# Residual of the output added in PSUM and copied out by ScalarE, TensorE conv in one band of three, first LN1 in large buffers

## The chip, the cores and the metric

The kernel runs on one core of a Trainium2 chip, in one launch. The metric is the device time in microseconds. The core has five engines that each run their own instructions in order: TensorE (PE; its weight loads are listed as PEld), VectorE (DVE), ScalarE (ACT), GpSimd (POOL) and SyncE (SP). Sixteen DMA engines carry all transfers, whichever engine issues them. SBUF is the large on-chip memory; PSUM holds the results of TensorE in banks of 512 float32 per partition.

## The reference

The input x has 16 images of 128 channels and 96 x 96 pixels, all in float32. One transformer block is computed, and the LN weights are ones and the biases zeros in the inputs given.

```python
xn1 = _layernorm(x_hwc, ln1_w, ln1_b)                  # over the 128 channels of each pixel
q, k, v = (xn1 @ w.T for w in (wq, wk, wv))            # 8 heads of 16 channels
q, k = _l2norm(q), _l2norm(k)                          # over the 9216 pixels
attn = softmax(einsum('bhcn,bhdn->bhcd', q, k) * 16 ** -0.5)
x = x + (attn @ v) @ wp.T                              # channel attention: 16 x 16 per head
xn2 = _layernorm(x_hwc, ln2_w, ln2_b)
h1 = einsum('bchw,oc->bohw', xn2, w_in)                # 1x1 conv, 128 -> 512 channels
h2 = conv3x3_depthwise(h1, w_dw)                       # each of the 512 channels by itself
x = x + einsum('bchw,oc->bohw', gelu(h2), w_out)       # 1x1 conv, 512 -> 128
```

## The kernel before

Channels lie on the 128 partitions, pixels along the free dimension. An image is cut into 8 bands of 12 rows (1152 pixels); a band has 3 units of 4 rows (384 pixels). The kernel works through 128 bands (16 images of 8), and g counts them.

First norm and attention. A band of x is loaded (`load`, L540, issued by SP). Four tiles of 128 pixels (a quad) are transposed on TensorE (`forth`, L602), VectorE takes the statistics (L609), POOL makes variance and power (L616, L620), ScalarE scales the tiles (L647) into a buffer zT. For the first image VectorE scales two of the four (L634). There are three zT buffers, each for one quad. From zT TensorE sums the Gram matrix of the image (`gram`, L661) and transposes the tiles back to channels (`back`, L692), which ScalarE places (`place`, L698). The attention of an image (L756 to L852) is a chain of small steps on the Gram matrix that ends in one 128 x 128 matrix. `mix` (L560) multiplies it with the normed image; the residual x is added by VectorE for the first bands (L566), else by ScalarE's copy-out (L569) and an accumulating DMA of x from memory (`add_x`, L572, issued by POOL). A second norm of the same kind gives the input of the FFN.

FFN. The 512 hidden channels are four chunks of 128. A chunk in the usual way is a job (`conv_job`): `hidden` (L877) makes 14 rows of the hidden layer by matmuls of 480 or 384 columns, ScalarE copies them out of PSUM (`kept`, L882), and the nine taps of the depthwise conv are shared. VectorE does most taps, one instruction each over 1152 pixels (`tap`, L895). Two or three taps are done as products on ScalarE (`product`, L890) that accumulating DMAs add up, first onto each other and then onto VectorE's sum (`add_products`, L899, issued by POOL); chunk 1 has three such taps, the others two. ScalarE applies the gelu (L903). In some bands chunk 3 goes another way (`by_matmuls`): TensorE does the whole conv as nine matmuls per unit with weights that hold hidden layer and tap together (L945), and ScalarE applies the gelu out of PSUM (L951). `by_pe` picks these bands: of the first 120 every second one (`PE_OF = 2`), of the last eight the six in `PE_LAST`.

`ffn_out` ends a band: four matmuls per unit add the chunks up in PSUM (`product`, L968), VectorE adds x (`add`, L975), and SP stores the band (L979).

The order of the work. Each step is given to a planner (`Plan`) with its engine, an estimated duration, the tiles it reads and writes, and a place. The planner plays the engines through in time: a free engine takes the ready step with the lowest place. The place is the number of the job in whose turn the step lies, plus a constant for its kind from the table `AT`, so a very negative constant means "as soon as it is ready" and a large one "when nothing else is". The order found is written out and each engine keeps to it. `T_ADD` and `T_MOVE` are the planner's costs of an accumulating and a plain transfer. Buffers: four PSUM banks `h` shared by hidden rows, mix, conv and output, five product buffers `pr`, ten `h3` (the sum of taps of one chunk of a band), six x bands of the second phase.

```python
PE_OF = 2
PR_BUFS, H3_BUFS, ZT_BUFS = 5, 10, 3          # from a longer line
T_ADD, T_MOVE = 3100, 1800
k = NG - 1 - g
return k in PE_LAST if k < NB else k % PE_OF in PE_BANDS
```

Of the kernel before, what the change touches and what calls it, by code (L numbers as in the profile page):

```python
# [18 lines left out]
BR = 12  # L19
PE_CHUNK = 3  # L20
PE_BANDS = (0,)
PE_OF = 2
PE_LAST = (0, 1, 2, 4, 5, 7)
TINY = 1e-20
UNIT_MIN = 1e-18
# [3 lines left out]
QT, QB = 4, 1  # L29
# [1 line left out]
X1_BUFS, XB_BUFS, PR_BUFS, H3_BUFS, ZT_BUFS = 2, 6, 5, 10, 3  # L31
IN_TURN = ("tr", "h3", "pr", "xb", "x1")
AT = dict(
    weights=86, zeros=34, load_a=-17.95, forth_a=-1.35, stats_a=-23.85, variance_a=50.15, power_a=-16.45,
    scaled_a=6.1, gram=-31.8, back_a=-145.85, place_a=68, attention=-19.55, mix=-17.6, residual=60.15,
    mixed=-98.2, add_x=-22.85, forth_b=-2, stats_b=-5.55, variance_b=52.05, power_b=-11, shift_b=-76.95,
    scaled_b=98.5, back_b=-23.15, place_b=20.55, halo=21.65, hidden=1.35, kept=-79.55, products=8.4,
    add_last=-64.4, tap=0.1, add_first=-14.5, gelu=-63.5, conv=1.15, conv_gelu=-1.85, out=4.9, add=-43.45,
    store=47.1,
)  # L40
STEP = dict(scaled=0.3, hidden=0.1, products=0.5, tap=0.166, conv=1.6, conv_tap=0.03, out=0.8, out_part=0.05)
SLACK = 300
NORM1_END = 6.0
EARLY = 5
WAIT = dict(POOL=350, SP=1300, ACT=1300)
T_WEIGHTS = 20000
T_VARIANCE = 420
T_POWER = 1000
T_ADD, T_MOVE = 3100, 1800


class Plan:
# [154 lines left out]
def tile_restormer_block(  # L207
# [136 lines left out]
    )  # L344
    op = plan.op

    def at(kind, place):
        return place + AT[kind]

    def bank(key, n=4 * P):  # L350

# [7 lines left out]
    def t_mm(n):  # L359
        return 2 * max(110, 0.84 * n)  # L360
# [10 lines left out]
    def pe(ns, p, f, r, w):  # L371
        op("PE", ns, p, f, r, w, ns + 200 + SLACK, ns)

    def dve(ns, p, f, r, w, two=False):
        op("DVE", ns, p, f, r, w, ns + 120 + SLACK, ns + 120, two=two)
# [29 lines left out]
    def weights(p):  # L405
# [14 lines left out]
            nc.scalar.dma_start(out=v["win"], in_=w_in.rearrange("(n p) c kh kw -> p n (c kh kw)", p=P))  # L420
            nc.scalar.dma_start(out=v["wout"], in_=w_out.rearrange("c j kh kw -> c (j kh kw)"))

        def transposed(parts, kept, gives):

            key = ("weights", next(names))
            h = ("h", key)
            d = {}

            def forth():
                d["pt"] = bank(key)  # L430
                for k, part in enumerate(parts()):
                    nc.tensor.transpose(d["pt"][:, k * P : (k + 1) * P], part, ident)

            pe(440, at("weights", p), forth, mine, [h])
            dve(700, at("weights", p), lambda: kept(d["pt"]), [h], [("w", g) for g in gives] + mine[1:])

        def keep_qkp(pt):
            nc.vector.tensor_copy(v["wqkT"], pt[:, : 2 * P])
# [53 lines left out]
        def unit_parts():  # L492
            for n in range(NCH):
                nc.vector.tensor_scalar(v["wt"][:, n, :], v["win"][:, n, :], unit[:, n : n + 1], None, ALU.mult)

        op("ACT", 400, at("load_a", p), loads, [], mine, T_WEIGHTS, dma=2 * T_MOVE)
        dve(1400, at("weights", p), units, [], [("w", "in")])
        dve(400, at("weights", p), shifts, [], [("w", "in"), ("w", "conv"), ("w", "shift")])
        transposed(
            lambda: [v["wqk"][:, :P], v["wqk"][:, P:], v["wp"], wv_sb], keep_qkp, ["qk"]  # L500
        )
        pe(440, at("weights", p), biases, [("w", "qk"), mine[1]], [("h", ("weights", "biases"))])
        dve(400, at("weights", p), lambda: nc.vector.tensor_copy(cqk, v["pc"]), [("h", ("weights", "biases"))], [("w", "qk")])
        pc = ("h", ("weights", "centred"))
        pe(1000, at("weights", p), centred, [("w", "qk"), mine[1]], [pc])
        dve(800, at("weights", p), keep_centred, [pc], [("w", "qk")])
        dve(700, at("weights", p), unit_parts, [mine[0], ("w", "in")], [mine[1]])
        transposed(
            lambda: [v["wt"][:, n, :] for n in range(NCH)],
            lambda pt: nc.vector.tensor_scalar(winT.rearrange("p n c -> p (n c)"), pt, w2, None, ALU.mult), ["in"],  # L510
        )
        transposed(
            lambda: [v["wout"][:, n * P : (n + 1) * P] for n in range(NCH)],
            lambda pt: nc.vector.tensor_copy(woutT.rearrange("p n c -> p (n c)"), pt), ["out"],
        )
        for t0 in (0, 4, 8):
            ts = range(t0, min(t0 + 4, 9))
            dve(170 * len(ts), at("weights", p), lambda ts=ts: comp_parts(ts), [mine[0]], [mine[1]])
            transposed(
                lambda ts=ts: [v["wt"][:, t % 4, :] for t in ts],  # L520
                lambda pt, ts=ts: nc.vector.tensor_scalar(
                    comp[:, ts[0] : ts[-1] + 1, :].rearrange("p t c -> p (t c)"), pt[:, : len(ts) * P],
                    w2, None, ALU.mult,
                ), ["conv"],
            )
# [18 lines left out]
    def norm(i, second, place_of):  # L544
# [8 lines left out]
        def x2(s, u):  # L553
            d = {}
            b = u // UPB
            loaded = x_key(i, b, False) == "xb"

            def mix():
                pm = d["pm"] = bank((name, u), UT)
                nc.tensor.matmul(rows(pm), lhsT=mats[i][0], rhs=interior(i, u), start=True, stop=True)  # L560
                if (i, b) not in xbs:
                    xbs[i, b] = xpool.tile([P, BR * W], F32, tag="x", name=f"x2_{i}_{b}")

            def residual():
                xt = x_unit(xbs, i, u)
                nc.vector.scalar_tensor_tensor(xt, d["pm"], mats[i][1], xt, ALU.add, ALU.add)  # L566

            def mixed():
                nc.scalar.activation(x_unit(xbs, i, u), d["pm"], AF.Identity, bias=mats[i][1])  # L569

            def add_x():
                nc.gpsimd.dma_start(out=xbs[i, b], in_=x_band(i, b), accum_op=ALU.add)  # L572

            pm = ("h", (name, u))
            ins = [z_unit(i, u), ("m", i)]
            if loaded:
                pe(t_mm(UT), at("mix", s), mix, [*ins, xtok(u)], [pm])
                dve(t_dve(UT), at("residual", s), residual, [pm], [xtok(u)])
                return
            pe(t_mm(UT), at("mix", s), mix, ins, [pm, xtok(u)])  # L580
            act(t_act(UT, 1) - 43, at("mixed", s), mixed, [pm], [xtok(u)])
            if u % UPB == UPB - 1:
                xb = [xtok(b * UPB + k) for k in range(UPB)]
                add(at("add_x", s), add_x, [], xb)

        def pixels(s, m):

# [2 lines left out]
            early = i == 0 and (not second or m < EARLY)  # L590
            key_ = "h" if early else "tr"
            by_dve = QT // 2 if early else 0

            def forth(q):
                if early:
# [28 lines left out]
                nc.vector.scalar_tensor_tensor(nb, d["mv"][:, :, 1], -1.0, d["rstd"], ALU.mult, ALU.mult)  # L624

            def zT(q):
                zTs[q] = zT_bufs[plan.slot["zT", (name, q)]]
                return zTs[q]

            def also_scaled(q):  # L630
# [35 lines left out]
            trs, bt = [(key_, (name, q)) for q in qs], ("batch", (name, m))  # L666
            for q, tr in zip(qs, trs):
                units = {t // TPU: None for t in range(q * QT, (q + 1) * QT)}
                pe(110 * QT, at("forth" + ab, s), lambda q=q: forth(q), [xtok(u) for u in units], [tr])
            for j in range(QB * QT // 2):  # L670
                dve(341, at("stats" + ab, s), lambda j=j: stats(j), [trs[2 * j // QT]], [bt])
            op("POOL", T_VARIANCE, at("variance" + ab, s), variance, [], [bt], T_VARIANCE + 33 + SLACK)
            op("POOL", T_POWER, at("power" + ab, s), power, [], [bt], T_POWER + 33 + SLACK)
            if second:
                dve(80, at("shift" + ab, s), shift, [], [bt])
            for h, (q, tr) in enumerate(zip(qs, trs)):
                zt, sh = ("zT", (name, q)), s + STEP["scaled"] * h
                if by_dve:
                    dve(by_dve * 240, at("scaled" + ab, sh), lambda q=q: also_scaled(q), [tr, bt], [(*zt, 0)])
                act((QT - by_dve) * (343 if second else 250), at("scaled" + ab, sh), lambda q=q: scaled(q), [tr, bt], [(*zt, 1)])  # L680
                if not second:
                    pe(QT * 220, at("gram", sh), lambda q=q: gram(q), [(*zt, 0), (*zt, 1), ("w", "ones")], [("g", i)])

        def channels(s, u):

# [23 lines left out]

            pb = ("bk", (name, u))  # L710
            quads = {(u * TPU + j) // QT: None for j in range(TPU)}
            pe(110 * TPU, at("back" + ab, s), back, [("zT", (name, q), k) for q in quads for k in range(2)], [pb])
            act(t_act(UT, 1) - 43 if second else t_copy(UT), at("place" + ab, s), place, [pb, ("w", "shift")], [z_unit(i, u)])
            for k, r, row, of in copies:
                act(225, at("place" + ab, s), lambda k=k, r=r, row=row: place_row(k, r, row), [pb, ("w", "shift")], [("z", k, of)])


        for u in range(0, NU if not second else 0, UPB):
# [240 lines left out]
    def ffn_out(p, g, s):  # L959
        i, b = divmod(g, NB)  # L960
        d = {}
        po = ("h", ("out", g, s))
        order = sorted(range(NCH), key=lambda n: (n != PE_CHUNK, n))

        def product(k, n):
            if k == 0:
                d["po"] = bank(("out", g, s), UT)
            nc.tensor.matmul(  # L968
                rows(d["po"]), lhsT=woutT[:, n, :], rhs=h3s[g, n][:, s * UR : (s + 1) * UR, :],
                start=(k == 0), stop=(k == NCH - 1),  # L970
            )

        def add():
            xt = x_unit(xbs, i, s + b * UPB)
            nc.vector.tensor_add(xt, d["po"], xt)  # L975

# [4 lines left out]
        for k, n in enumerate(order):  # L981
            pk = p + STEP["out_part"] * k
            pe(t_mm(UT), at("out", pk), lambda k=k, n=n: product(k, n), [("h3", (g, n), s), ("w", "out")], [po])
        dve(t_dve(UT), at("add", p), add, [po], [("xb", (i, b), s)])
        if g == NG - 1:
            move(at("store", p), lambda: store(s, 1), [("xb", (i, b), s)], [], T_MOVE / UPB)
        elif s == UPB - 1:
            move(at("store", p), lambda: store(0, UPB), [("xb", (i, b), k) for k in range(UPB)], [], T_MOVE)

    def by_pe(g):  # L990
        k = NG - 1 - g
# [61 lines left out]
```

## Time and profile before

| what | value |
|---|---|
| time, median of 3 runs | 4176.35 us (4175.98 to 4178.71) |
| profiled execution | 4194.94 us, its span 4193.2 us |
| mean granted TensorE clock | 0.998 |
| PE, DVE, ACT, POOL busy | 99%, 97%, 88%, 62% of the span |
| moved by DMA | 827.63 MB, mean 197 GB/s |
| VectorE's additions of x (L975) | 384 of 558 ns |
| ScalarE's copies of hidden rows (L882, 384 columns) | 1118 of 508 ns |

The profile is one execution. Busy shares are averages over lead-in, steady work and tail. A row of the groups gives line, engine, operation, output and inputs, the count, then busy time and mean duration of one, then the idle time of the engine before them and what ended it. The duration of an instruction on TensorE, VectorE and ScalarE contains a part that the next instruction overlaps, so the pace of a run of equal instructions is read from their starts. A float32 matmul appears as two MATMUL rows. A share of the DMA queues is that of the time of all 16 engines.

### The profile page before, as it was taken

What the parts mean: (1) busy time and instruction counts of PE and PEld (TensorE: products, weight loads), DVE (VectorE), ACT (ScalarE), POOL (GpSimd) and SP (SyncE); (2) the same over time, 40 slices, a digit from 0 to 9 for tenths busy, and PEclk for the clock granted to TensorE, in tenths of its full rate; (3) what the DMA queues carried; (4) which work ended last, traced back from release to release, by engine and by line L of the source; (5) the groups of instructions that cost most, each with busy time, mean ns of one, the idle gap of its engine ahead of it and who ended that gap; (6) DMA issues with size and microseconds to landing.
All of it is one profiled execution on the core that took longest, in us unless ns stands there. A gap on an engine that the chain in (4) does not pass through costs nothing. (4 is left out here: it accounts for less than half of the span.)

```text
span 4193.2 us, 52283 instructions
## 1 busy us (share of the span) xinstructions
PE 4151.7 (99%) x17457; PEld 2684.0 (64%) x17457; DVE 4073.2 (97%) x4676; ACT 3682.0 (88%) x6970; POOL 2593.8 (62%) x2373
## 2 busy tenths in 40 slices
PE   8999999999999999999999999999999999999999
PEld 6666666666666666666666666666666666666565
DVE  6999999999999999999999999999999999999998
ACT  4988989899899888999988899898998989889885
POOL 3656666566675666657666566656656667565542
PEclk9999999999999999999999999999999999999999
DMA  2999999999999999999999999999999999999997
GB/s 78 192 191 201 208 198 208 189 213 201 206 207 204 206 196 204 203 202 207 198 206 198 197 206 198 206 201 201 208 197 212 195 207 202 191 205 199 196 197 160
DMA packets 203934, 827.63 MB, mean 197 GB/s; under 512 B 23568, under 2 KB 24976, under 8 KB 203664
## 3 DMA queue, kind: packets, MB, share of 16 engines
q0 software_dynamic: 164160, 672.47, 82.9%
q1 hardware_dynamic: 37152, 151.01, 9.8%
q8 instruction: 138, 2.26, 0.2%
q10 hardware_dynamic: 2352, 0.81, 0.1%
q14 instruction: 132, 1.08, 0.1%
HBM read 148.26 MB, written 75.50 MB: 53 GB/s over the span
## 5 line engine op out<-in xcount | busy, mean ns | idle before, releaser
L895 DVE SCALAR_TENSOR_TENSOR h<-h,ratio,h 128x1152 f32<-128x1152 f32 x2104 | 2933.0, 1415 | 5.0
L890 ACT ACTIVATE pr<-h,ratio 128x1152 f32<-128x1152 f32 x1018 | 1304.2, 1290 | 21.8 <-DMA pr<-pr 20.3
L945 PE MATMUL h<-xn,comp 128*128 128x384 f32 x3564 | 1277.4, 486 | 1.7 <-ACT h L951 0.9
L968 PE MATMUL h<-h,woutT 128*128 128x384 f32 x3072 | 1112.8, 487 | 1.8 <-ACT h L903 0.7
L877 PE MATMUL h<-xn,winT 128*128 128x384 f32 (+1 forms) x2676 | 1048.4, 500 | 2.1 <-DVE x L975 1.1
L945 PEld LDWEIGHTS h<-xn,comp 128*128 128x128 f32 x3564 | 647.3, 189 | 394.4 <-issue 10.4
L899 POOL DMA_DIRECT2D pr<-pr x573 | 545.7, 960 | 475.1 <-ACT pr L890 325.7
L968 PEld LDWEIGHTS h<-h,woutT 128*128 128x128 f32 x3072 | 560.7, 190 | 345.1 <-issue 7.5
L882 ACT COPY h<-h 128x384 f32<-128x384 f32 (+1 forms) x1338 | 658.1, 521 | 139.7 <-PE h L877 122.4
L877 PEld LDWEIGHTS h<-xn,winT 128*128 128x128 f32 x2676 | 479.5, 190 | 290.9 <-issue 49.7
L899 POOL DMA_DIRECT2D h<-pr x445 | 433.9, 977 | 356.7 <-DVE h L895 93.7
L895 DVE SCALAR_TENSOR_TENSOR h<-h,ratio 128x1152 f32<-128x1152 f32 x446 | 630.1, 1419 | 11.5 <-ACT h L882 7.8
L903 ACT ACTIVATE h<-h 128x1152 f32<-128x1152 f32 x448 | 533.7, 1192 | 51.9 <-DMA h<-pr 48.0
L616 POOL TENSOR_SCALAR ve_b<-st_b 128x4 f32<-128x4 f32 x288 | 364.3, 1265 | 310.8 <-DVE st_b L609 304.6
L620 POOL TENSOR_TENSOR rstd_b<-ve_b,mhalf 128x4 f32<-128x4 f32 x288 | 525.1, 1823 | 13.9
L620 POOL TENSOR_TENSOR rstd_a<-ve_a,mhalf 128x4 f32<-128x4 f32 x288 | 498.2, 1730 | 15.7 <-POOL ve_a L616 0.2
L616 POOL TENSOR_SCALAR ve_a<-st_a 128x4 f32<-128x4 f32 x288 | 323.9, 1125 | 292.2 <-DVE st_a L609 291.7
L651 ACT ACTIVATE zT<-pT_b,nb_b,rstd_b 128x128 f32<-128x128 f32 x1132 | 431.4, 483 | 45.7 <-DVE nb_b L624 45.4
L647 ACT ACTIVATE zT<-pT_a,rstd_a 128x128 f32<-128x128 f32 x1080 | 314.7, 398 | 39.3 <-POOL rstd_a L620 38.4
L661 PEld LDWEIGHTS g<-zT 128*128 128x128 f32 x2304 | 294.4, 192 | 50.0 <-ACT zT L647 7.9
L661 PE MATMUL g<-zT 128*128 128x129 f32 x2304 | 307.1, 276 | 3.3 <-ACT zT L647 3.3
L560 PE MATMUL h<-xn,mwT 128*128 128x384 f32 x768 | 283.5, 490 | 1.2 <-ACT x L569 0.8
(172 smaller groups left out, 3605.4 us busy)
## 6 DMA issues: line engine op xcount, KB each, us to landing
pr<-pr POOLq DMA_DIRECT2D x573, 576.0 KB, 6.9
h<-pr POOLq DMA_DIRECT2D x445, 576.0 KB, 7.4
x<-in_x_dram SPq DMA_DIRECT2D x128, 576.0 KB, 6.5
out_dram<-x SPq DMA_DIRECT2D x127, 576.0 KB, 5.6
x<-in_x_dram POOLq DMA_DIRECT2D x122, 576.0 KB, 7.7
out_dram<-x SPq DMA_DIRECT2D x3, 192.0 KB, 1.9
weights<-in_L_conv_w_in_dram ACTq DMA_DIRECT2D x1, 256.0 KB, 10.7
weights<-in_L_conv_w_out_dram ACTq DMA_DIRECT2D x1, 256.0 KB, 11.6
```

The source lines that it names most:

```text
L616: nc.gpsimd.tensor_scalar(ve, d["mv"][:, :, 2], 1.0 / C, EPS, ALU.mult, ALU.add)
L620: nc.gpsimd.tensor_tensor(rstd, d["ve"], mhalf, ALU.pow)
L651: nc.scalar.activation(zT(q)[:, k, :P], d["pT", q][:, k, :], AF.Identity, bias=d["nb"][:, t : t + 1], scale=d["rstd"][:, t : t + 1],)
L661: nc.tensor.matmul(grams[i][:, : P + 1], lhsT=zt[:, :P], rhs=zt, start=(q == 0 and k == 0), stop=(q == NU * TPU // QT - 1 and k == QT - 1),)
L877: nc.tensor.matmul(rows(ph), lhsT=winT[:, n, :], rhs=window(xn, r0 + r, e - r, 1), start=True, stop=True)
L882: nc.scalar.copy(window(h1_, r, e - r, 1), rows(d.pop(("ph", r))))
L890: nc.scalar.activation(to, shifted(t), AF.Copy, scale=ratio[:, n, t : t + 1])
L895: nc.vector.scalar_tensor_tensor(h3, shifted(t), ratio[:, n, t : t + 1], onto, ALU.mult, ALU.add)
L899: nc.gpsimd.dma_start(out=to, in_=d["pr", t], accum_op=ALU.add)
L903: nc.scalar.activation(h3, h3, AF.Gelu)
L945: nc.tensor.matmul(d["pc"], lhsT=comp[:, t, :], rhs=window(xn, r0 + dy, UR, dx), start=(t == 0), stop=(t == 8),)
L968: nc.tensor.matmul(rows(d["po"]), lhsT=woutT[:, n, :], rhs=h3s[g, n][:, s * UR : (s + 1) * UR, :], start=(k == 0), stop=(k == NCH - 1),)
```

## The change

1. The output's residual: for all bands but the last two, a fifth matmul adds x in PSUM, with the identity as weights, and ScalarE copies the sum out of PSUM over x. In the last two bands VectorE adds as before.
2. `PE_OF` goes from 2 to 3.
3. The first image's LN1: zT lies in the `h3` buffers (two quads in one) and not in the three zT buffers; POOL writes the column of ones in each.
4. The table of places is new: constants of their own for the first image (`_0`), for the load of the weights (`load_w`) and for the weights that the FFN needs (`late`). The planner's costs of transfers and of the weights' load are changed.

```diff
-PE_OF = 2
+PE_OF = 3
...
 AT = dict(
-    weights=86, zeros=34, load_a=-17.95, forth_a=-1.35, stats_a=-23.85, variance_a=50.15, power_a=-16.45,
...
-    add_last=-64.4, tap=0.1, add_first=-14.5, gelu=-63.5, conv=1.15, conv_gelu=-1.85, out=4.9, add=-43.45,
-    store=47.1,
+    load_w=-4.75, weights=-31.7, zeros=-128.5, load_a=-128.95, forth_a=-3.9, stats_a=-14.85, variance_a=359.5,
...
+    scaled_b=-72.8, back_b=-10.8, place_b=-110.1, res=-6.15,
+    evict_x=-72.85, halo=194.05, hidden=1.65, kept=27.1, products=9.4, add_last=-104.1, tap=7.9, add_first=7.45,
+    gelu=237.8, conv=0.8, conv_gelu=6.8, out=5.2, add=-34.55, store=254.3, mix_0=-15.9, residual_0=351.3,
...
-T_WEIGHTS = 20000
+T_WEIGHTS = 12000
...
-T_ADD, T_MOVE = 3100, 1800
+T_ADD, T_MOVE = 3060, 1640
...
             def zT(q):
-                zTs[q] = zT_bufs[plan.slot["zT", (name, q)]]
+                if q in zTs:
+                    return zTs[q]
+                if not apart:
+                    zTs[q] = zT_bufs[plan.slot["zT", (name, q)]]
+                    return zTs[q]
+                two = [k for k in (q - q % 2, q - q % 2 + 1)]
+                t = h3p.tile([P, BR * W], F32, tag="h3", name=f"zT_{two[0]}")
+                for k in two:
+                    zTs[k] = t[:, k % 2 * QT * (P + 1) : (k % 2 + 1) * QT * (P + 1)].rearrange("p (t c) -> p t c", c=P + 1)
+                    nc.gpsimd.memset(zTs[k][:, :, P:], 1.0)
                 return zTs[q]
...
+        by_pe_ = g < NG - 2
...
-                start=(k == 0), stop=(k == NCH - 1),
+                start=(k == 0), stop=(k == NCH - 1 and not by_pe_),
             )
 
-        def add():
+        def residual():
+            xt = x_unit(xbs, i, s + b * UPB)
+            nc.tensor.matmul(d["po"], lhsT=ident, rhs=xt, start=False, stop=True)
+
+        def evict_x():
+            nc.scalar.copy(x_unit(xbs, i, s + b * UPB), d["po"])
+
+        def add_here():
...
-        dve(t_dve(UT), at("add", p), add, [po], [("xb", (i, b), s)])
+        if by_pe_:
+            xt = ("xb", (i, b), s)
+            pe(t_mm(UT), at("res", p), residual, [xt], [po])
+            act(t_copy(UT), at("evict_x", p), evict_x, [po], [xt])
+        else:
+            dve(t_dve(UT), at("add", p), add_here, [po], [("xb", (i, b), s)])
```

## The prediction, made before the change was run

> **What bounds the kernel now.** I read the page's busy shares first. Three engines and the DMA are near full, so the shares alone decide nothing; I then cut the span into lead-in, middle and tail (columns: length, busy time of PE, PEld, DVE, ACT, POOL, granted clock, DMA share, GB/s).
>
> ```profile
> PE 4151.7 (99%) x17457; PEld 2684.0 (64%) x17457; DVE 4073.2 (97%) x4676; ACT 3682.0 (88%) x6970; POOL 2593.8 (62%) x2373
> ...
> q0 software_dynamic: 164160, 672.47, 82.9%
> q1 hardware_dynamic: 37152, 151.01, 9.8%
> ```
>
> ```profile
> 0.00:20.00 20.00, 8.88 (x46) 8.14 (x47) 7.72 (x32) 3.94 (x10) 6.45 (x24) 1.00 0.82 276
> 20.00:160.00 140.00, 129.16 (x710) 95.74 (x710) 113.18 (x222) 95.69 (x216) 70.48 (x107) 0.94 0.41 89
> 160.00:4150.00 3990.00, 3973.98 (x16582) 2557.20 (x16581) 3919.18 (x4394) 3566.14 (x6724) 2511.76 (x2237) 1.00 0.95 202
> ```
>
> In the middle TensorE idles 16 us of 3990, VectorE 71, ScalarE 424. TensorE sets the pace. Busy time of pipelined matmuls needs a check, so I read starts in the timeline of a middle stretch:
>
> ```profile
> 1004.22 2.42 PE L877 MATMUL h<-xn,winT 128*128 128x480 f32 x6
> 1006.48 2.10 PE L968 MATMUL h<-h,woutT 128*128 128x384 f32 x6
> 1008.41 1.45 PE L945 MATMUL h<-xn,comp 128*128 128x384 f32 x4
> 1009.70 0.49 PE L692 MATMUL pB_a<-ident,zT 128*128 128x128 f32 x3
> 1010.02 1.06 PE L661 MATMUL g<-zT 128*128 128x129 f32 x8
> ```
>
> Six 384-wide passes take 1008.41-1006.48 = 1.93 us, 0.322 each (the 486 ns of a row is latency). The first line holds the six passes of one 14-row band (four 480-wide, two 384-wide): 2.26 us. A 128-wide pass takes about 0.11. All passes: 9640 of 384 columns x 0.322 = 3104, 440 of 480 columns x 0.404 = 178, 6912 of 128 x 0.11 = 760, some 460 small ones of attention about 85: 4127 us, so the 4152 busy are truly filled.
>
> The Trainium skill (Perfetto Trace Analysis, Identifying the Most-Contended Engine) says that matmul busy time misjudges TensorE and that the share of weight loads should be used instead; that share is 64% here, and by it work taken off TensorE would be worth nothing (about 4170 us, the lead-in alone). The passes counted above say otherwise, and the measurement decides.
>
> **The change on TensorE.** Each matmul is two passes. Conv by TensorE falls from every second to every third of the first 120 bands: 60 to 40, 20 bands less (the last eight keep their six). Per band 9 taps x 3 units x 2 = 54 passes: -1080 x 0.322 = -348. Those bands' chunk 3 now needs its hidden rows: +20 x 2.26 = +45. The identity product: 126 bands x 3 units x 2 = 756 passes x 0.322 = +243. I take two passes, as the mix product L560 has (768 for 384 units), not one as the transposes have; one would make it 122 less. It waits for its x band, which the second norm has read long before. Sum **-60 us** on the path.
>
> **VectorE.** The addition L975 goes 378 times; next starts follow it by 0.46 us where I looked: -174. Twenty jobs of six taps come: a tap paces at (4.07-1.41)/2 = 1.33 us, +160. Sum -14: 3905 of the middle, nowhere the bound.
>
> ```profile
> 1008.56 4.07 DVE L895 SCALAR_TENSOR_TENSOR h<-h,ratio,h 128x1152 f32<-128x1152 f32 x3
> ```
>
> **ScalarE.** The copy-out is a form that the trace has (L698, 128x384 out of PSUM):
>
> ```profile
> L698 ACT COPY xn<-pB_a 128x384 f32<-128x384 f32 x384 | 194.7, 507 | 73.9 <-PE pB_a L692 72.9
> L890 ACT ACTIVATE pr<-h,ratio 128x1152 f32<-128x1152 f32 x1018 | 1304.2, 1290 | 21.8 <-DMA pr<-pr 20.3
> L951 ACT ACTIVATE h<-h 128x384 f32<-128x384 f32 x198 | 102.4, 517 | 44.2 <-PE h L945 43.8
> ```
>
> Back to back it paces at 0.37 us: 378 x 0.37 = 140 (192 by the row's mean). A moved band adds two products (1.15 each by starts), a gelu (1.07) and three evictions of hidden rows (1.24), and loses three conv gelus (0.39 each): 3.4 x 20 = 69. Sum +209: 3775 of the middle, 95%. Its 424 idle us are the cover. It frees every PSUM bank that TensorE fills in the FFN, and it runs in order: behind a late copy-out stand hidden-row evictions and products, and TensorE waits for banks. From below nothing (the copies fit the idle), from above half of the added 209 as TensorE waits; I take 5, since TensorE lost only 16 us in all with ScalarE at 89%.
>
> **DMA.** Each moved band adds two accumulating DMAs (products 1 and 2 of a two-tap job): 40. One costs 82.9% of 4193.2 / 1140 = 3.05 us of all 16 engines: **+122 us**. All queues hold 93.1% of the span, 3904 us; lead-in 16+57 and tail 23 taken off, the middle holds 3807, a share of 0.954. After: 3929. POOL issues them (some 0.97 us each, +39 on an engine at 62%); in POOL's queue the variance and power steps stand behind them, and the next norm waits for those.
>
> So in the middle TensorE needs 3974-60+16 = 3930 us if its idle stays, and DMA needs 3929 us if it never idles. The two meet. What DMA can hold is read from 50 us windows (three of eighty here, the same columns):
>
> ```profile
> 1260.00:1310.00 50.00, 50.00 (x192) 31.25 (x192) 49.36 (x61) 45.16 (x82) 24.66 (x25) 1.00 0.91 193
> 1310.00:1360.00 50.00, 50.00 (x198) 31.68 (x197) 49.60 (x55) 44.83 (x79) 28.99 (x27) 1.00 1.01 213
> 1360.00:1410.00 50.00, 50.00 (x216) 32.57 (x216) 49.06 (x54) 44.69 (x86) 34.75 (x30) 1.00 0.99 202
> ```
>
> Windows run from 0.85 to 1.02, and stretches at 1.00 go on without TensorE losing anything, so 0.95 is demand and not a ceiling. Middle by sustained share: 1.00 gives 3929 (-61), 0.9925 gives 3959 (-31), 0.985 gives 3989 (no gain), 0.975 gives 4030 (+40). I take 0.9925, halfway between full and break-even, because a fed queue shows 0.99 to 1.02, while five product buffers limit how much can be queued: median landing is already 6.9 to 7.4 us against 4.9 in the lead-in.
>
> [...]
>
> **Lead-in.** The first image's LN1 fills TensorE (19.60 of 20 us from 20 to 40: per quad 4 transposes, 8 Gram passes, 4 transposes back). Large buffers don't make passes cheaper; they let the 72 back-transposes (7.9 us) stand outside the chain to attention, whose serial steps at 51 to 66 us they can then fill. VectorE's first tap is at 97.3 us, the first accumulation at 102. Gain between 8 and -5 (ones columns written per buffer on POOL, and the weights hold two of ten buffers, so the last two quads wait for a release); I take -6 us. It is worth having for DMA too, which idles until then.
>
> **Other edits.** Every place in the order is changed, and the planner's transfer costs: 16 us of TensorE idle can be won, and nothing in the trace bounds the loss; nought is taken. Stores now wait for ScalarE, and x loads stand behind them on SP; that queue waits for buffers anyway, at no cost unless a copy-out is over a microsecond late.
>
> **Sum.** Profiled execution 4194.94 (span 4193.2 and 1.7 around it). Middle -31 (the 5 us of ScalarE waits lie inside DMA's limit), lead-in -6: 4158. The median is 0.9956 of the profiled time: 4176.35 - 37 x 0.996 = **4140 us**.
>
> **The rivals.**
> - TensorE alone sets the pace, DMA finds its room: middle 3930+5, lead-in -6: 4176 - 61 = 4115. For it: TensorE 99.6% full with VectorE at 98.2% beside it now. Against: DMA would be at 0.998.
> - DMA becomes the bound below 0.985, slower than before: its place is the chain of two or three dependent accumulations that each hold a product buffer; ScalarE's next product waits, and in order behind it everything that frees banks. At 0.975: 4176 + 40 - 6 = 4210. It decides from a sustained 0.985 downwards, 0.981 with the lead-in's gain. For it: gelu already waits 48.0 us for `h<-pr` and products 20.3 for `pr<-pr`. Against: these are small beside 3990.
> - ScalarE at 95% makes TensorE wait for banks by 55 us of the upper 105: the gain is gone, about 4170.
> - The reordering loses what the sums give; it has no row, and is in the range's upper end.
>
> **How the numbers follow.** Within 0.2% (8.4 us, about what this measurement can tell from none) is 4168 to 4184.7. Forecast (DMA and TensorE together, 0.987 to 0.997): 0.52, faster. TensorE alone: 0.18, faster. DMA below break-even: 0.20, of it 0.15 slower and 0.05 same. ScalarE or the order: 0.10, of it 0.02 faster, 0.05 same, 0.03 slower. Faster 0.72, same 0.10, slower 0.18. Low end: TensorE alone, with the 5 us of waits not lost and a lead-in of -11, 4176 - 71 = 4105. High end: a share of 0.978 (4017, +27), lead-in -3, 4200.
>
> **What would show it.** Right: 2484 conv passes, a new group of 756 identity passes, TensorE's total some 60 us lower, DMA share in the middle 0.98 or more, ScalarE about 95%, first tap some 6 us earlier. Wrong: a share that stays near 0.95 with TensorE idle after ScalarE (banks), gelu or products waiting hundreds of microseconds for DMA, an accumulation dearer than 3.05 us, or identity passes unlike 0.322 us.

## The result, and the profile after

The changed kernel takes 4220.39 us (4215.93 to 4222.51), the kernel before, run beside it, 4176.16 us (4175.24 to 4178.71). The ratio is 1.0103, 95% interval 1.0091 to 1.0115: slower by 44 us where 36 us faster was forecast, and above the high end of 4200.

The busy shares and DMA queues of the page after:

```profile
PE 4126.0 (98%) x17253; PEld 2645.1 (63%) x17253; DVE 4065.8 (96%) x4418; ACT 3871.2 (92%) x7408; POOL 2606.5 (62%) x2431
...
q0 software_dynamic: 169920, 696.07, 84.7%
q1 hardware_dynamic: 37152, 151.01, 10.0%
```

The pass count is the forecast one: 17457 - 1080 + 120 + 756 = 17253. VectorE has 258 instructions less but hardly less time. Now the same cuts as before (columns as there):

```profile
20.00:160.00 140.00, 130.88 (x759) 97.09 (x758) 117.81 (x225) 101.83 (x231) 72.65 (x110) 0.99 0.48 106
160.00:4150.00 3990.00, 3921.98 (x16256) 2502.38 (x16255) 3893.80 (x4125) 3733.74 (x7123) 2516.20 (x2267) 1.00 0.97 206
```

For comparison the kernel before must be taken from a second profiled execution. The first (4194.94 us) lies 18 us above the median of its runs; the second, of the run `before_again` below, has a span of 4174.8 us. The same stretch there:

```profile
160.00:4150.00 3990.00, 3981.77 (x16626) 2566.74 (x16625) 3930.24 (x4403) 3581.28 (x6734) 2482.49 (x2240) 1.00 0.96 202
```

TensorE was busy for all but 8 us of this middle; after, it idles 68 us, although ScalarE and DMA still show room (3734 of 3990, 0.97).

Busy time alone understates this, since after each interruption a matmul shows its whole 0.49 us, of which a run of them adds only 0.322 each. So I count TensorE's lost time: start of the last pass, minus start of the first, minus all passes at the prediction's paces (4127 us of work before, 4127 - 60 = 4067 after).

| kernel | TensorE work | first to last pass start | lost |
|---|---|---|---|
| before, first profile | 4127 | 5.6 to 4189.2 | 57 |
| before, second profile | 4127 | 5.4 to 4170.7 | 38 |
| after | 4067 | 5.6 to 4213.9 | 141 |

From the second profile of before to after, 60 us of work went and 103 us of lost time came: +43, the measured difference. What had to be found is where 103 us of waiting come from.

### The profile page after: what moved, and what is told of

It reads as the page before. It is cut to its first block, busy times and chain, and to the rows that moved or that the text cites. A ratio compares the mean times of both kernels' runs of the same rounds, so it can differ in the third digit from the quotient of the medians.

```text
span 4218.0 us, 52196 instructions
## 1 busy us (share of the span) xinstructions
PE 4126.0 (98%) x17253; PEld 2645.1 (63%) x17253; DVE 4065.8 (96%) x4418; ACT 3871.2 (92%) x7408; POOL 2606.5 (62%) x2431
## 3 DMA queue, kind: packets, MB, share of 16 engines
q0 software_dynamic: 169920, 696.07, 84.7%
## 4 chain that ended last, share of the span: by engine, by line
PE 54%; DVE 25%; ACT 12%; DMA 4%; POOL 3%; issue 2%; ACTq 0%; POOLq 0%; DVEq 0%
DVE h L917 22%; PE h L991 14%; PE h L967 12%; PE h L899 11%; ACT pr L912 4%; PE h L998 3%; PE g L677 3%; PE h L566 3%; DMA h<-pr 2%; ACT h L904 2%; PE pB_a L714 2%; PE pB_b L714 2%; PE pT_a L609 2%; PE pT_b L609 2%; ACT zT L667 2%
## 5 line engine op out<-in xcount | busy, mean ns | idle before, releaser
L917 DVE SCALAR_TENSOR_TENSOR h<-h,ratio,h 128x1152 f32<-128x1152 f32 x2204 | 3053.7, 1408 | 9.7
L912 ACT ACTIVATE pr<-h,ratio 128x1152 f32<-128x1152 f32 x1058 | 1391.7, 1320 | 40.9 <-DMA h<-pr 20.2
L967 PE MATMUL h<-xn,comp 128*128 128x384 f32 x2484 | 871.2, 486 | 2.5 <-ACT h L904 1.2
L991 PEld LDWEIGHTS h<-h,woutT 128*128 128x128 f32 x3072 | 561.1, 191 | 369.0 <-ACT h L904 23.1
L904 ACT COPY h<-h 128x384 f32<-128x384 f32 (+1 forms) x1398 | 700.7, 562 | 44.1 <-PE h L899 38.0
L921 POOL DMA_DIRECT2D h<-pr x465 | 473.5, 1025 | 274.7 <-DMA pr<-pr 61.5
L967 PEld LDWEIGHTS h<-xn,comp 128*128 128x128 f32 x2484 | 451.2, 189 | 281.5 <-issue 14.2
L925 ACT ACTIVATE h<-h 128x1152 f32<-128x1152 f32 x468 | 578.7, 1241 | 9.9 <-DMA h<-pr 8.0
L627 POOL TENSOR_TENSOR rstd_a<-ve_a,mhalf 128x4 f32<-128x4 f32 x288 | 538.1, 1869 | 13.8 <-POOL ve_a L623 0.2
L623 POOL TENSOR_SCALAR ve_b<-st_b 128x4 f32<-128x4 f32 x288 | 311.3, 1081 | 286.9 <-DVE st_b L616 268.8
L998 PE MATMUL h<-x,ident 128*128 128x384 f32 x756 | 306.1, 487 | 0.0
```

The lines of the kernel that those rows point to most:

```text
L623: nc.gpsimd.tensor_scalar(ve, d["mv"][:, :, 2], 1.0 / C, EPS, ALU.mult, ALU.add)
L627: nc.gpsimd.tensor_tensor(rstd, d["ve"], mhalf, ALU.pow)
L904: nc.scalar.copy(window(h1_, r, e - r, 1), rows(d.pop(("ph", r))))
L912: nc.scalar.activation(to, shifted(t), AF.Copy, scale=ratio[:, n, t : t + 1])
L917: nc.vector.scalar_tensor_tensor(h3, shifted(t), ratio[:, n, t : t + 1], onto, ALU.mult, ALU.add)
L921: nc.gpsimd.dma_start(out=to, in_=d["pr", t], accum_op=ALU.add)
```

## How a stall travels: one stretch of the trace after

Rows of the timeline after, by engine (start, duration, engine, line; in brackets the idle time before it and its releaser). First ScalarE:

```profile
1710.90 1.35 ACT L925 ACTIVATE h<-h 128x1152 f32<-128x1152 f32 x1
1711.97 1.43 ACT L912 ACTIVATE pr<-h,ratio 128x1152 f32<-128x1152 f32 x1
1713.11 0.65 ACT L904 COPY h<-h 128x384 f32<-128x384 f32 x1
```

TensorE meanwhile, with the weight load of the pass that waits:

```profile
1711.62 0.81 PE L899 MATMUL h<-xn,winT 128*128 128x384 f32 x2
1713.82 0.94 PEld L991 LDWEIGHTS h<-h,woutT 128*128 128x128 f32 x4 [2.00 <-ACT h L904]
1713.82 1.56 PE L991 MATMUL h<-h,woutT 128*128 128x384 f32 x4 [1.38 <-ACT h L904]
...
1717.48 0.60 PE L609 MATMUL pT_b<-ident,x 128*128 128x128 f32 x4
```

And VectorE:

```profile
1709.50 5.76 DVE L917 SCALAR_TENSOR_TENSOR h<-h,ratio,h 128x1152 f32<-128x1152 f32 x4
1718.11 0.76 DVE L616 BATCH_NORM_STATS2 st_b<-pT_b 128x6 f32<-128x256 f32 x2 [2.85 <-PE pT_b L609]
```

TensorE needs the hidden rows' PSUM bank back, but ScalarE does a gelu (L925) and a product (L912) before the eviction (L904). TensorE stands 1.38 us (its weight load 2.00, in the same wait); the transposes written after it come that much later; VectorE, whose next instruction is the statistics of these transposes, stands 2.85 us. A VectorE that is 97.6% busy in the middle (3893.80 of 3990) has little room to win 2.85 us back. Its taps feed the sums to which ScalarE applies the gelu, so a late tap can come back to TensorE through ScalarE; this stretch doesn't show the return, and how many stalls run this way was not counted.

## The experiments

All ratios are to the kernel before, run beside it on the same chip; times are medians, and gains are differences of ratios times 4176 us, so that chips with slightly different baselines compare. In the expectations that speak of several limits at once (called theory C in some), TensorE, VectorE, ScalarE and DMA hold one written order together, so that relief of any single one hardly shows. The rivals are one engine or the DMA as the bound, and the planner's transfer costs (theory P in some).

**The baseline again.** `before_again` is the kernel before, unaltered.

> The kernel before the change, unaltered, for a second profiled execution: the first one took 4194.9 where the median is 4176, so its trace may hold some 18 us that its usual execution has not. All theories: 4174 to 4190, TensorE 99% busy, its waits on ScalarE some 110 us by the table of waits.

4177.11 us, ratio 0.9998 (0.9989 to 1.0007): ten executions resolve about 0.1%, some 4 us; the four of most runs below about 0.15 to 0.2%, 6 to 8 us. A gain against after, a difference of two ratios, is uncertain by some 7 to 10 us.

**One relief at a time, order kept.** The planner is told nothing, so every instruction stays where it was; a part of the work is left out.

```diff
# less_dma: 41 of 593 accumulations of one product onto another
+            if n == PE_CHUNK and t != DMA_TAPS[0] and jobs_3.index(g) % 2:
+                return
# less_act: 8 of the copy-out's 384 columns
-            nc.scalar.copy(x_unit(xbs, i, s + b * UPB), d["po"])
+            nc.scalar.copy(x_unit(xbs, i, s + b * UPB)[:, :8], d["po"][:, :8])
# less_pe: identity product in one unit of three
+            if s == 2:
                 nc.tensor.matmul(d["po"], lhsT=ident, rhs=xt, start=False, stop=True)
# less_dve: chunk 3's taps after the first on 9 of 12 rows
+            r = 9 if n == PE_CHUNK and t != left[0] else BR
```

> The changed kernel with its order kept, but in every second usual-way job of chunk 3 the accumulation of the second product is left out (41 accumulating DMAs fewer, so as many as before the change; one tap is lost there). Theory D (the DMA engines' share has a ceiling and the 40 added accumulations sit on it): 41 x 3.05 = 125 us of DMA go, the DMA share in the middle falls to about 0.95, and the time falls from 4220 to 4150 or lower. Theory S (ScalarE's copy-outs are what TensorE waits for): within 8 us of 4220. Theory C (all engines are so full that the fixed order loses everywhere): 5 to 25 us faster.

> The changed kernel with its order kept, but ScalarE copies only 8 of the 384 columns of each output unit out of PSUM (the rest of the output stays x without the FFN): 378 x 376 x 0.83 ns = 118 us of ScalarE go. Theory S: PSUM banks come free sooner and the time falls by 40 us or more, to 4180 or lower. Theory D: within 8 us of 4220. Theory C: 5 to 25 us faster.

> The changed kernel with its order kept, but the identity product is left out for units 0 and 1 of each band (the residual is missing there): 252 x 0.645 = 163 us of TensorE go. If TensorE is still what sets the pace, as it did before the change, the time falls by 100 us or more, to 4120 or lower. Theory D and theory S both say within 10 us of 4220, since TensorE only waits for others. Theory C: 15 to 60 us faster.

> The changed kernel with its order kept, but in the usual-way jobs of chunk 3 the five taps after the first run over 9 of 12 rows (part of the conv is lost): 82 x 5 x 288 x 1.07 ns = 126 us of VectorE go. Theories D and S: within 8 us of 4220. If VectorE, 97.6% busy in the middle, is the bound, 50 us or more faster. Theory C: 5 to 25 us faster.

| run | taken away, expected | us | ratio, 95% | gain against after |
|---|---|---|---|---|
| less_dma | 125 us DMA | 4216.23 | 1.0095 (1.0080 to 1.0110) | 3 |
| less_act | 118 us ScalarE | 4221.61 | 1.0104 (1.0089 to 1.0119) | 0 |
| less_pe | 163 us TensorE | 4206.55 | 1.0079 (1.0059 to 1.0099) | 10 |
| less_dve | 126 us VectorE | 4209.78 | 1.0077 (1.0062 to 1.0092) | 11 |

Only the last two are gains, at the edge of what the intervals separate, and each returns a tenth or less of what it takes away. (By busy time less went than expected: 111 us of the accumulations' queue, 95 of ScalarE, 108 of VectorE.) This fits no single bound. It fits theory C's own ranges only in part: less_dve lies in its 5 to 25 us, less_dma (5 to 25), less_act (5 to 25) and less_pe (15 to 60) fall short of theirs. ScalarE's row is the surprise: in the table of waits it ends 67.5 us of idle time of TensorE's matmuls (14.4 in the second profile of before) and 203.1 us of its weight loads' (70.8), more than any other engine. The two sums overlap, as in the stretch above, so they don't add up to lost time. Yet less ScalarE work leaves TensorE's lost time at 141.

**All four, and all but one.** `less_all` has the four edits above together; each `all_but_` run leaves one of them out; `less_pe_dve` has two.

> The changed kernel with its order kept and all four reliefs at once: 41 accumulations, most of each ScalarE copy-out, two of three identity products and a quarter of the rows in chunk 3's later taps left out (125, 118, 163 and 126 us of DMA, ScalarE, TensorE and VectorE; each alone gave 0 to 14 us). Theory C (the engines are limits together, so that only relief of all of them shows): 80 us or more faster, 4140 or lower. Theory L (the written order with its buffers and delays between engines is itself the limit, not any amount of work): less than 50 us faster, 4170 or higher.

> The kernel after with its order kept, and the reliefs of VectorE, ScalarE and DMA, with every identity product issued (the output is not the reference's in the relieved places). TensorE is busy 3922 of the middle's 3990 us with all of its passes, so it can win 70 us at most: if TensorE bounds with the others 4170 to 4210. Rival, its 98% is only waiting in another form: 4105 to 4140.

> The kernel after with its order kept, and the reliefs of TensorE, ScalarE and DMA, with all taps whole (the output is not the reference's in the relieved places). VectorE is busy 3894 of the middle's 3990 us: if it bounds with the others 4170 to 4210. Rival, VectorE follows the others: 4105 to 4140.

> The kernel after with its order kept, and three of the four reliefs: identity product for one unit in three (-163 us of TensorE), nine rows of twelve in chunk 3's later taps (-126 us of VectorE), every second second-accumulation of chunk 3 left out (-125 us of DMA); ScalarE's copy-outs stay whole (the output is not the reference's in these places). Four limits together: ScalarE at 92% holds the order, more than half of the 115 us of the four reliefs is lost, 4160 to 4195. Rival, ScalarE's load is no limit (its own relief gave nothing): 4105 to 4125.

> The kernel after with its order kept, and the reliefs of TensorE, VectorE and ScalarE, with all accumulations issued (the output is not the reference's in the relieved places). If DMA (share 0.97 of the middle) bounds with the others: 4170 to 4210, since the transfers still need 3870 us of the middle's 3990. Rival, DMA only follows: 4105 to 4130, and the middle's DMA share goes to 0.99 or more.

> The kernel after with its order kept and two reliefs: identity product for one unit in three (-163 us of TensorE), nine rows of twelve in chunk 3's later taps (-126 us of VectorE); ScalarE and DMA carry their whole load (the output is not the reference's in the relieved places). Singly these two gave 14 and 11 us. If TensorE and VectorE are the pair that holds this order, they must bring most of the 115 us of all four: 4135 to 4165. Rival, at least three reliefs are needed: 4185 to 4200.

| relieved | us | ratio, 95% | gain against after |
|---|---|---|---|
| all four | 4105.43 | 0.9841 (0.9819 to 0.9862) | 109 |
| VectorE, ScalarE, DMA (not TensorE) | 4198.38 | 1.0045 (1.0030 to 1.0060) | 24 |
| TensorE, ScalarE, DMA (not VectorE) | 4198.92 | 1.0045 (1.0029 to 1.0062) | 24 |
| TensorE, VectorE, DMA (not ScalarE) | 4136.22 | 0.9894 (0.9880 to 0.9909) | 87 |
| TensorE, VectorE, ScalarE (not DMA) | 4131.56 | 0.9884 (0.9869 to 0.9898) | 91 |
| TensorE, VectorE | 4154.81 | 0.9938 (0.9921 to 0.9955) | 69 |

All four together give what theory C asked for, 80 us or more. The rest is the answer to which limits. Without TensorE's relief, or without VectorE's, four fifths of the 109 us is lost; without ScalarE's or DMA's, a fifth. TensorE and VectorE are two separate limits of this order that lie at nearly the same time: with everything else relieved, each alone still gives some 4198 us, 19 us above the kernel before. (Of the rest, ScalarE's 4136 lies between its two forecasts, DMA's 4132 next to the range of the rival.) The middle without TensorE's relief, then without VectorE's:

```profile
160.00:4150.00 3990.00, 3932.32 (x16324) 2517.32 (x16324) 3802.75 (x4137) 3655.07 (x7142) 2477.22 (x2232) 1.00 0.95 201
```

```profile
160.00:4150.00 3990.00, 3844.46 (x15813) 2415.65 (x15812) 3902.28 (x4133) 3631.92 (x7141) 2525.05 (x2231) 0.99 0.95 201
```

The first kernel does all of TensorE's work with VectorE, ScalarE and DMA relieved, and still loses 120 us of TensorE (5.6 to 4192.4 less 4067), 82 more than the second profile of before (63 more than the first). So of the 103 us that came, some 21 go with those three reliefs, and 82 stay with this order kept. The chain that ended last shows the two by name. Without TensorE's relief, then without VectorE's:

```profile
PE 81%; ACT 10%; DVE 3%; DMA 3%; issue 2%; POOL 2%; ACTq 0%; POOLq 0%; DVEq 0%
```

```profile
DVE 65%; PE 14%; ACT 7%; DMA 5%; POOL 5%; issue 3%; ACTq 0%; POOLq 0%; DVEq 0%
```

In the kernel after, the chain changes hands between them:

```profile
PE 54%; DVE 25%; ACT 12%; DMA 4%; POOL 3%; issue 2%; ACTq 0%; POOLq 0%; DVEq 0%
```

ScalarE and DMA are a second layer: nothing that can be measured from after's state (0 and 3 us), but 22 and 18 us once the two in front are relieved (69 to 91 and to 87). `less_pe_dve` also shows what DMA can hold:

```profile
160.00:4150.00 3990.00, 3868.81 (x15940) 2434.34 (x15939) 3822.84 (x4157) 3752.78 (x7169) 2481.19 (x2277) 0.99 0.98 208
```

The DMA share is 0.98 (0.99 up to 4050 us): the DMA can run near full when it is asked to.

**The places and buffers without the swap of work.** `big_only` is after with TensorE's conv in every second band and VectorE's addition, as before; the new table of places, large buffers and planner's costs stay. `old_places_new_lead` puts, in `big_only`, the steady-state places back to those of before; only the first image, the weights, zeros, the first loads and attention keep the new ones.

```diff
# both
-PE_OF = 3
+PE_OF = 2
-        by_pe_ = g < NG - 2
+        by_pe_ = False
# old_places_new_lead, in AT (among others)
-    ... hidden=1.65, kept=27.1, products=9.4, add_last=-104.1, tap=7.9, gelu=237.8, ...
+    ... hidden=1.35, kept=-79.55, products=8.4, add_last=-64.4, tap=0.1, gelu=-63.5, ...
```

> The changed kernel with two of its parts undone: VectorE adds x to the output as before and TensorE has the conv in one band of two; the large buffers of the first LN1, the new table of places and the planner's new costs stay. If the loss comes from the identity product with the moved bands (theories D, S, C): the lead-in's gain of 10.5 us is seen alone, 4160 to 4172. If the new table or the large buffers are at fault (theory T): 4190 to 4220.

> The work of big_only (VectorE adds x, TensorE conv in one band of two, large buffers in the first LN1), but the places of the steady part are those of the kernel before; only the first image's places, those of the weights, load_a, zeros and attention are the new ones. If the new steady places cost what big_only lost (theory T): 4155 to 4175, so 25 to 45 below big_only and 5 to 20 below the kernel before, from the lead-in. If the large buffers or the first image's places cost it: 4190 to 4205 like big_only.

4201.89 us, 1.0050 (1.0035 to 1.0065), and 4186.13 us, 1.0022 (1.0012 to 1.0031). The first is as theory T said, the second lies in neither of its two ranges. If the parts add up, the 43 us (0.0103 x 4176) split: 9 for all that `old_places_new_lead` keeps (large buffers, the places of first image, weights and attention, the planner's costs; 0.0022), 12 for the steady-state places (0.0050 - 0.0022), 22 for the swap of work on top (0.0103 - 0.0050), which was to bring 31. With the old work, then, places, buffers and planner's costs lose 21 us; that they lose as much with the swapped work is not shown. How far each kernel was behind the second profile of before, in us, at the last output pass of a band:

| band | 7 | 31 | 63 | 111 | 119 | 127 |
|---|---|---|---|---|---|---|
| old_places_new_lead | -3.3 | 0.4 | 2.2 | 10.0 | 7.8 | 8.3 |
| big_only | 9.9 | 10.7 | 17.3 | 32.7 | 23.3 | 23.9 |
| after | -3.4 | 3.6 | 25.2 | 40.8 | 31.7 | 43.2 |

At the end of the first image (band 7) two of the three are 3 us ahead and `big_only` is 10 behind. The first profile of before is itself 7 us behind the second there, so this is no more than two executions differ by (against the first, after is 10.5 us ahead: the 10.5 us in the expectation of `big_only`). By band 31 the lead is gone. The 8 us of `old_places_new_lead` come after band 63, long after the large buffers were in use, so an order that differs in the steady part too is as good a cause as the buffers. After loses through the middle, at no single place; it wins 9 back before band 119 and loses 11 in the last eight bands.

**The identity product alone.** `of2_res_pe` has identity product and copy-out, but the conv on TensorE in every second band as before.

```diff
-PE_OF = 3
+PE_OF = 2
```

> One part without the other: the identity product and the copy-out by ScalarE, but TensorE has the conv in one band of two as before. TensorE then has 756 more passes and none fewer: 243 us by 0.322 each on the engine that set the pace. 4176 - 10 + 243 = 4410, 4390 to 4440. If an identity pass cost half, or were hidden, 4290 or less.

4435.75 us, 1.0610 (1.0589 to 1.0631). Its busy shares and the group of the new passes:

```profile
PE 4391.9 (99%) x18213; PEld 2825.2 (64%) x18213; DVE 3987.0 (90%) x4298; ACT 3853.3 (87%) x7348; POOL 2515.6 (57%) x2391
...
L998 PE MATMUL h<-x,ident 128*128 128x384 f32 x756 | 305.9, 486 | 0.0
```

Against `big_only` it is 234 us more for 756 passes, 0.31 each, near the forecast 0.322 us. And the copy-outs, all 378 of them on ScalarE, do no harm by themselves: TensorE's lost time here (5.6 to 4430.2 less 4370 of work) is 55 us, less than the 62 us of `big_only` (5.7 to 4194.6). All others have more room here than after: VectorE is busy 90% of the span, ScalarE 87%, and the DMA share of the middle is 0.90; the run doesn't say whose room it is that helps. The second half of the swap, from every second band to every third, takes 303 us off TensorE (-348 + 45) and returned 212 (1.0610 to 1.0103); VectorE is back at 96% and TensorE's lost time at 141. So it is this half that fails to pay: its missing 91 us are more than the 43 that the kernel loses.

**Other orders of the same work.** `tadd_2900` tells the planner that an accumulation is cheaper, which changes the order; `less_dma_planned` leaves out the 41 accumulations of `less_dma` and lets the planner know. `old_descended` has other constants in the table, found from those of before in steady work; the parenthesis in its expectation is a slip: no work is left out.

```diff
# tadd_2900
-T_ADD, T_MOVE = 3060, 1640
+T_ADD, T_MOVE = 2900, 1640
# less_dma_planned
+            if n != PE_CHUNK or jobs_3.index(g) % 2 == 0:
                 add(at("add_last", j), ...)
# old_descended, in AT (among others)
-    ... kept=27.1, products=9.4, add_last=-104.1, tap=7.9, gelu=237.8, res=-6.15, evict_x=-72.85, ...
+    ... kept=-14.51, products=138.01, add_last=-637.92, tap=0.15, gelu=332.98, res=4.86, evict_x=68.08, ...
```

> The changed kernel, all work the same, but the planner is told 2900 ns for an accumulating transfer and not 3060, so it writes out another order in which DMA is less of a limit. Theory P (the order was squeezed by the planner's own DMA limit, the chip has room): 20 us or more faster, 4200 or lower. Theory D (the chip's DMA is the limit): within 10 us of 4220 or slower, up to 4260, with more waits on accumulations.

> As less_dma (41 accumulations of chunk 3 left out, one tap lost in each of those jobs), but the planner knows it and writes out an order for it. Theory D and P in one (DMA, real or planned, is what the order is built around; less_dma showed nothing since its order was the old one): 25 us or more faster than 4220, 4195 or lower. Theory C (all engines too full, whichever): within 15 us of the 4216 of less_dma.

> The work of the kernel after unaltered (four bands' worth of it exact: conv by TensorE in one band of three, identity products, copy-outs, large buffers), in another order: constants for the places that start from those of the kernel before in steady work. If the order that after has is what loses the gain of the swap: 4130 to 4175. If the work itself meets the limits of TensorE and VectorE whatever the order: 4190 to 4235, like after and the order of tadd_2900.

4232.10 us, 1.0129 (1.0112 to 1.0146); 4226.24 us, 1.0108 (1.0093 to 1.0123); 4241.33 us, 1.0146 (1.0131 to 1.0161). A cheaper price for transfers does not help, and an accumulation measures 84.7% of 4218.0 us / 1180 = 3.03 us, near the 3.06 the planner assumes: theory P falls. The order with 41 accumulations less planned for is no faster than `less_dma`, and `old_descended` lies above both of its ranges. No other order of the whole work came below after's. Three orders are not all orders: whether one exists that keeps the 60 us is open.

**A smaller dose.** `half_tuned` has the conv on TensorE in two bands of five (of the first 120: 48, where before has 60 and after 40), identity product and copy-out in every second band, and another table.

```diff
-PE_BANDS = (0,)
-PE_OF = 3
+PE_BANDS = (0, 2)
+PE_OF = 5
-        by_pe_ = g < NG - 2
+        by_pe_ = g < NG - 2 and g % 2 == 0
```

> Half of the change with places of its own: TensorE conv in two bands of five (54 bands, 46 in the changed kernel, 66 before), identity product in every second band (63 bands), large buffers. TensorE has 12 x 15.1 - 63 x 1.93 = 60 us less, as much as in the changed kernel, for 24 accumulations more (73 us) and not 40, and 110 us of ScalarE and not 209. Theories C and D: 4150 to 4172, faster than both kernels. Theory L (it hangs on the order alone, and the planner's orders miss the chip's by 30 to 60 us): 4165 to 4195.

4178.40 us, 1.0003 (0.9994 to 1.0012): no difference. On TensorE it saves what after saves (12 bands less: -209 + 27, 378 passes more: +122; -60), with 24 accumulations added for 40 and about half of the addition to ScalarE, and loses 102 us (5.7 to 4174.2 less 4067) where before loses 38. VectorE is busy 4071 us, as before (4072), with TensorE's work now level with it. The time lies in the range of theory L, that it hangs on the written order, and above that of theories C and D: halving the added load did not bring the 60 us out. This is the best of the tried versions that compute everything, and it does not beat before.

## Why the prediction was wrong

**What held.** The pass count and the identity pass at 0.322 us; TensorE's work, 60 us less; VectorE's load in the middle, 3905 forecast, 3894 measured, and ScalarE's, 3775 and 3734; the tap at 1.41 us a row; the accumulation at 3.05 (3.03). The lead-in's 6 us can't be told from the 7 us by which two executions of before differ there.

**The steps that failed: "Sum -14: 3905 of the middle, nowhere the bound" and "3930 us if its idle stays".** The forecast needed both, for VectorE and for TensorE, and each failed by itself at the same height.

VectorE: the number was right and the conclusion wrong. The working compared each resource with the length of the middle, as if an engine at 97.9% of it had 2.1% to give. A middle of 3959 us leaves VectorE 54 us of idle, less than the 71 of the profile shown, while its partners are rearranged around it. In `all_but_dve`, with everything but VectorE relieved, it still idles 88 us of the middle (3902 busy) and the kernel takes 4199 us: that is VectorE's limit in this order, and all that was taken off TensorE, ScalarE and DMA buys nothing below it.

TensorE: the idle of 16 us and the 5 us for waits on ScalarE were far too small. Lost time went from 38 to 141 us, which eats the 60 us of saved work and 43 more. In `all_but_pe`, with VectorE, ScalarE and DMA relieved, 120 us of it remain and the kernel takes 4198 us. The forecast saw two limits that meet (TensorE and DMA) and missed the pair that decides (TensorE and VectorE).

**Why TensorE loses more is open in part.** In before its work exceeds VectorE's busy time by 55 us (4127 against 4072), after the two are level (4067 and 4066). That neither can then make up for the other's stalls fits `half_tuned` (4067 and 4071, 102 us lost) and `of2_res_pe` (4370 and 3987, 55 lost). It doesn't fit `all_but_pe`, where TensorE has 110 us more than VectorE (4067 and 3957) and still loses 120: there the order is one written for level loads, and ScalarE's instructions stand in it as before. Whether an order written for that work would lose less was not run.

**DMA's sustained share, 0.9925.** The share reached 0.97, and the rival "DMA below 0.985" would have read it as the cause. It is not the first limit: 125 us less DMA alone brings 3 us, and with TensorE and VectorE relieved DMA runs at 0.98 to 0.99. After's share is what the others ask for. That rival gave nearly the right time (4210) with the wrong mechanism, so by luck. (Its break-even with the lead-in's gain is 3929 of 3996, 0.983 and not 0.981; nothing else rests on it.)

**ScalarE, "I take 5".** The 103 us of added lost time are about the "upper 105" of that rival, and ScalarE ends most of the waits. Still ScalarE's load costs nothing by itself from there: `less_act` gives 0. Its instructions stand between the two full engines, as the stretch above shows, so a wait on ScalarE can be the form in which others' lateness reaches TensorE. What part of the 103 us comes from ScalarE's longer queue, what from VectorE's lack of room and what from the order was not separated. The Trainium skill (Perfetto Trace Analysis, Optimization Strategies under Optimizing DMA Performance) advises, where matmul idles on others, to optimise the engines that block the critical path. Read as the engine that ends most of TensorE's waits, ScalarE, the advice would have led astray here: its work was cut by some 95 us of busy time to no effect.

**"Other edits: nought is taken".** With the old work the steady-state places cost 12 us (`big_only` against `old_places_new_lead`), and buffers, first places and planner's costs 9 where -6 was forecast. If these add to the swap, two thirds of the miss of 79 us (forecast -36, measured +43 by the ratio) is the swap's (-31 forecast, +22 measured: 53) and the rest these two (9 + 6, and 12). The rival named reordering had no price in it, and 0.10 was too little for it.

## What to carry to other kernels

Before counting a gain on the fullest engine, ask what the second fullest keeps: with TensorE at 99.6% of the middle and VectorE at 98%, there was little to win on TensorE alone, and a new written order lost more than that to stalls. To tell limits from followers, relieve all suspects at once with the order kept, then leave one relief out at a time: single reliefs summed to 24 us here where all four gave 109. The engine that ends most waits, or a DMA share of 0.97, need not be the limit.

## What was not expected of the hardware

Two profiled executions of the same program (before) differ by 18 us of span, 4193.2 and 4174.8, and nearly all of that is TensorE's lost time, 57 and 38 us: a baseline for trace comparisons needs more than one execution. In the kernel after, stretches in which TensorE stalls can also show a lower granted clock, as around an image's attention, though not always:

```profile
1700.00:1725.00 25.00, 23.10 (x94) 13.57 (x93) 16.86 (x19) 25.00 (x53) 15.36 (x14) 1.00 0.98 202
...
2025.00:2050.00 25.00, 21.96 (x94) 14.34 (x93) 24.35 (x39) 23.63 (x53) 19.32 (x18) 0.86 1.01 221
```

The mean clock went from 0.998 to 0.995, some 13 us of 4218 if all of it counted, and to 0.991 in `all_but_dve`, where TensorE has less work; no run separates this from the waits. The first line holds the stretch shown above: ScalarE is busy 25 of 25 us, TensorE 23.1 and VectorE 16.9.
